# Quarter times in the scheduler of a woven attention kernel, and two tokens to a partition

## The chip, the core and the metric

The kernel runs on one core of one Trainium2 chip. It is one launch, and the metric is the device time of that launch in microseconds (us). The time before is 2787.61 us, the median of three runs (2787.22 to 2788.68).

A core has five engines that run side by side and meet at semaphores: TensorE (PE) multiplies matrices and writes to PSUM, VectorE (DVE) and ScalarE (ACT) do elementwise work and read PSUM, GpSimd (POOL) does elementwise work in SBUF, and SyncE (SP) issues DMAs here. The program fixes the order of the instructions of each engine.

## What is computed

The input `x` has 16 batches of 256 tokens of width 256. Four steps are added to it one after the other, each preceded by a conditioning step:

```python
x = x + attn0(cond(x, fside, fside, braak_embed, stage))     # cross attention, then 16 heads of width 16, causal
x = x + ffn0(cond2(x, category, W, b))                       # own weight per batch, then fp4-quantized gate/up/down
x = x + attn1(diffuse(x, zX, zY, zR))                        # reaction-diffusion, then 16 heads of width 64
x = x + moe(cond2(x, expert, ...))                           # MLP, then 8 experts, top 2, and a shared one

def diffuse(y, zX, zY, zR):                # y: tokens x features, edges reflected
    lap_x = y[:, left] - 2 * y + y[:, right]          # along the features
    lap_y = y[above, :] - 2 * y + y[below, :]         # along the tokens
    return zX * lap_x + zY * lap_y + zR * y * (1 - y)
```

`attn0` rotates queries and keys and takes the softmax of 256 x 256 causal scores per head. `attn1` first normalizes each token, then works in two segments of 128 tokens; each head has 16 extra keys and values beside the 128 of its segment. All is in fp32.

## The kernel before

The program has two parts. `woven` covers everything up to `attn1`; `mixture` covers the experts and isn't touched by the change.

**Streams.** In `woven`, each stage is a Python generator (`stage_a`, `stage_e`, `stage_f`, `stage_g`, `stage_p`, `stage_d`, `stage_v` and some that prepare weights). A generator yields operations in its own order; it can also yield a condition on the counters in `g.done` ("batch b has left stage D"), or a `Want`, a request for one of the free PSUM tiles. There are four `single` tiles of one bank and two `pair` tiles of two banks. The stages work on different batches at the same time:

- `stage_a`: cross attention, the projection of queries, keys and values (`project_heads`), and `heads_maximum`, which finds each query's largest score and stores it in `qpad`.
- `stage_e`: `heads_exponential` (scores again, with the maximum folded in, and the exponential into `b_e`), `heads_values`, then the output projection through `b_oT`, added to `x`.
- `stage_f`: the quantized feed-forward. `stage_d`: `diffuse`, the normalization and the transposed tokens `e_zT`.
- `stage_p`: projections of `attn1` for four heads at a time. `stage_g`: `scores4`, their scores and softmax into `f_prob`. `stage_v`: `values4`, the weighted values into `f_oT` and their projection, added to `x`.

**The planner.** `weave` runs while the program is built. It keeps, for each engine, the time at which it will be free, and for each tile when it was last written and read. In each turn it looks at the next operation of every stream, works out when it could start (`ready`), and issues the earliest one; ties go to the stream that stands first in the list (a, e, gate, up, down, f, g, p, d, v). The costs are constants in the code, such as `COSTS`, and for TensorE the formulas in `Unit.cost`. An operation of TensorE from another stream than the last one counts as 0.1 us later (`TURN`), so that a stream keeps TensorE while it has work ready. So the planner fixes the order of each engine's instructions; the chip's semaphores decide when they run.

**Narrow products.** TensorE's array has 128 rows. Most products use all of them ("wide"). Three groups contract over 32 rows or fewer ("narrow"), and their operands lie in one of four quarters of the rows, 0 to 31, 32 to 63 and so on:

- the maximum group of `heads_maximum`: 4 products into `pair` from `b_qkT`, 16 rows
- the exponential group of `heads_exponential`: 4 products into `pair` from `b_qS` and `b_qkT`, 17 rows
- the score group of `scores4`: 8 products into `pair` from `keys` and `f_q`, 32 rows

Each group handles two heads, so two quarters in turn: `j0 = 0` is quarters 0 and 1, `j0 = 2` quarters 2 and 3. Per batch there are eight groups of each kind. Each takes one of the two `pair` tiles and gives it back when VectorE and ScalarE have read it. The planner before gives a narrow product a cost of `max(0.155, t / 2)` and treats TensorE as one resource.

Products that write 32 or 64 columns (`heads_values`, the values in `values4`) are a third kind. An fp32 product appears as two MATMUL records in the trace.

**Tokens.** A batch of `x` lies in SBUF as `[128, 2, 256]`: partition p holds token p and token 128 + p. `diffuse` computes the token Laplacian as a product with a 256 x 256 table `lap`: for each half of the tokens, two wide products of 256 columns. `copy_` offers an operation to ScalarE and to VectorE, whichever the planner finds earlier.

In the profile, nearly all instructions of the woven part bear L162, the line in `Unit` that makes the call; they are told apart by the tiles that they write and read.

Of the kernel before, what the change touches and what calls it, by code (L numbers as in the profile page):

```python
# [19 lines left out]
P = 128  # L20
# [106 lines left out]
HOP = 0.15  # L127
LANDING = 4.5
TURN = 0.1
GAP = 0.6  # L130
# [6 lines left out]
def row_size(ap):  # L137
    return math.prod(ap.shape[1:])


# [7 lines left out]
class Unit:  # L148
# [17 lines left out]
    def cost(self, fn, outs, ins):  # L166
        if self.name == "SP":
            return 0.06
        if self.name == "PE":
            if fn == "transpose":  # L170
                return 0.12
            lhsT, rhs = ins
            rows, cols, t = lhsT.shape[0], row_size(lhsT), row_size(rhs) / 570

            if rows <= 64:
                return max(0.155 if rows <= 32 else 0.19, t / 2)
            return max(t / 3.5, 0.08) if cols <= 32 else max(t / 2, 0.13) if cols <= 64 else t
        fixed, each = COSTS[self.name]
        n = max(row_size(x) for x in outs[:1] + ins)
        if fn == "reciprocal":  # L180
            each = 0.006
        return fixed + each * n + (0.3 if len(outs) > 1 else 0)


def weave(streams):
# [4 lines left out]
    free, written, read, rings = {}, {}, {}, {}  # L190
    turn = None
    names = lambda aps: [x.tensor.name for x in aps]

    def ready(op, engine):
# [4 lines left out]
        for x in op.outs:  # L199
# [7 lines left out]
            for p in before:  # L207
                if p and not p[1] == engine == "SP":
                    t = max(t, p[0] + (HOP if p[1] != engine else 0.0))
        return t  # L210

    def issue(op, choice, start):
        engine, cost, call = choice
        free[engine] = start + cost
        end = start + cost + (LANDING if engine == "SP" else 0.0)
        for n in names(op.ins):
            if end > read.get(n, (0.0, engine))[0]:
                read[n] = (end, engine)
# [13 lines left out]
    while waiting:  # L232
        best, moved = None, False
        for rank, w in enumerate(waiting):
# [15 lines left out]
            for c in op.choices:  # L250
                start = max(ready(op, c[0]), free.get(c[0], 0.0))
                if c[0] == "PE" and w is not turn:
                    start += TURN
                key = (start + (GAP if op.filler else 0.0), rank, c[1])
                if best is None or key < best[0]:
                    best = (key, w, c, start)
        waiting = [w for w in waiting if w[0] is not None]
        if best is not None:
# [4 lines left out]
            else:  # L263
                issue(w[1], c, start)
                if c[0] == "PE" and not w[1].filler:
                    turn = w
            w[1] = None
# [127 lines left out]
def stage_e(g):  # L395

    for b in range(g.B):
# [16 lines left out]
        for c in range(2):  # L414
            for st in range(2):
                yield g.pe.transpose(pt[:, c, st * P : (st + 1) * P], o[:, st, c * P : (c + 1) * P], g.ident)
        yield copy_(g, oT, pt)
        g.singles.append(both)
# [5 lines left out]
        g.singles.append(both)  # L424
        g.done["A"] = b + 1


def fetch_a(g, b):
# [11 lines left out]
    yield g.sp.dma_start(out=f, in_=a["fside_BxSxS_0"][b].rearrange("(c p) d -> p c d", p=P))  # L440
    yield g.sp.dma_start(out=g.x[b], in_=a["x"][b].rearrange("(c p) d -> p c d", p=P))

# [370 lines left out]
def stage_p(g):  # L813
    k, a = g.k, g.a
    yield lambda: g.done["A"] > 0 and g.done["W"] == 3
    g.lap, op = load(g, g.w, "lap", [P, 2, S], a["lap"])
    yield op
    g.z = []
    for n in ("condB_zX", "condB_zY", "condB_zR"):
        t, op = load(g, g.w, n, [P, g.B], a[n].unsqueeze(0).to_broadcast([P, g.B]))  # L820
        g.z.append(t)
        yield op
    g.gn, op = load(g, g.w, "g", [P, 2], a["g"])
    yield op
# [60 lines left out]
def diffuse(g, b):  # L885

    zx, zy, zr = (z[:, b : b + 1] for z in g.z)
    y = g.x[b]
    one = yield from single(g, y)
    ply = one.rearrange("p (s d) -> p s d", s=2)  # L890
    for st in range(2):
        yield from mm_(g, ply[:, st, :], [(g.lap[:, c, st * P : (st + 1) * P], y[:, c, :]) for c in range(2)])
    lx, u = tile_l(g, [P, 2, D], "e_lx"), tile_l(g, [P, 2, D], "e_u")
    yield g.pool.tensor_tensor(lx[:, :, 1 : D - 1], y[:, :, 0 : D - 2], y[:, :, 2:D], ALU.add)
    yield g.pool.tensor_tensor(lx[:, :, 0:1], y[:, :, 1:2], y[:, :, 1:2], ALU.add)
    yield g.pool.tensor_tensor(lx[:, :, D - 1 : D], y[:, :, D - 2 : D - 1], y[:, :, D - 2 : D - 1], ALU.add)
    yield g.dve.tensor_scalar(u, y, -1.0, 1.0, ALU.mult, ALU.add)
    yield g.dve.scalar_tensor_tensor(u, y, zr, u, ALU.mult, ALU.mult)
    yield g.dve.scalar_tensor_tensor(lx, y, -2.0, lx, ALU.mult, ALU.add)
    yield g.dve.scalar_tensor_tensor(u, lx, zx, u, ALU.mult, ALU.add)  # L900
# [15 lines left out]
    for c in range(2):  # L916
        yield g.act.activation(zT[:, c, :], pt[:, c, :], AF.Copy, scale=g.gn[:, c : c + 1])
    g.singles.append(one)
# [48 lines left out]
def stage_v(g):  # L967

    for i in range(4 * g.B):
# [4 lines left out]
        if n == 3:  # L974
            yield g.sp.dma_start(out=g.k.xd[b].rearrange("(s p) d -> p s d", p=P), in_=g.x.pop(b))
            g.done["L"] = b + 1
# [37 lines left out]
def values4(g, n, b, prob, pm, v, wo):  # L1014
# [19 lines left out]
    oT = tile_l(g, [P, 2, S], "f_oT", 2)  # L1034
    yield copy_(g, oT, po)
    g.singles.append(one)
    if n % 2 == 1:
# [3 lines left out]
        for st in range(2):  # L1041
            yield g.pe.transpose(pt[:, st * P : (st + 1) * P], pm[:, st].rearrange("p j n -> p (j n)"), g.ident)
        yield copy_(g, ppT, pt)
        g.singles.append(one)
# [508 lines left out]
```

## Time and profile before

| | |
|---|---|
| median of the runs | 2787.61 us |
| the profiled execution | 2794.98 us |
| its span, first to last instruction | 2793.3 us |
| woven part, to the last projection of `attn1` | about 1799 us |
| TensorE busy | 2701.6 us (97%) |
| VectorE, ScalarE, GpSimd busy | 1434.2, 934.3, 856.5 us |
| MATMUL records | 15999 |
| mean granted TensorE clock | 0.977 |
| `x,lap` products: records, mean | 128, 381 ns |
| `keys,f_q`: records, mean | 2048, 294 ns |
| `b_qkT` into `pair`, both widths: records | 1024 |
| `b_qS,b_qkT`: records | 1024 |
| `f_oT` copies on ScalarE: count, median | 59, 585 ns |

Busy times of TensorE overlap and their ends are modelled, so work on TensorE is best read from the distance between the starts of instructions. A row of a timeline gives the start in us from the beginning, the modelled time to the end of the last one in the row, the engine, the line, the operation, what is written and read, the rows and columns used, the shape that streams through, and the count. A row of groups gives the shapes, the count, the total time and the mean of one, and then the engine's idle time before them and what ended it.

### The profile page before, as it was taken

The numbers are of one execution on the slowest core, as the hardware profiler recorded it, in microseconds if no ns is written. First come the engines' busy times: TensorE is split into PE (matmuls) and PEld (weight loads), VectorE is DVE, ScalarE is ACT, GpSimd is POOL, SyncE is SP. The second block draws the span as 40 slices with busy tenths as digits, with TensorE's granted clock in tenths as the row PEclk, the third lists the DMA queues.
The fourth block names the chain that finished last, engine by engine and source line by source line (L and its number), as shares of the span: only waits on it lengthen the run. The fifth ranks groups of instructions, "written<-read, shape, count | busy, mean of one in ns | idle before, by whom it ended". The sixth has DMA issues, their size and how long they took to land. (4 is left out here: it accounts for less than half of the span.)

```text
span 2793.3 us, 42335 instructions
## 1 busy us (share of the span) xinstructions
PE 2701.6 (97%) x15999; PEld 2045.2 (73%) x15999; DVE 1434.2 (51%) x3113; ACT 934.3 (33%) x2418; POOL 856.5 (31%) x1030
## 2 busy tenths in 40 slices
PE   7999999999999999999999999799999999999999
PEld 5666777777777777777777778555566888888866
DVE  6456776776776776776777776433340000000023
ACT  2223334333333333333333334333222222222221
POOL 4323344434444334334434344223330000000035
PEclk7879999999999999999999999899999999999999
DMA  3122032322222222222221223241112455555523
GB/s 113 58 65 87 25 99 83 94 72 70 94 73 71 93 73 71 93 74 69 93 75 64 77 83 95 75 125 50 50 39 74 139 195 193 187 196 198 198 84 106
DMA packets 196526, 270.39 MB, mean 97 GB/s; under 512 B 34912, under 2 KB 167264, under 8 KB 186976
## 3 DMA queue, kind: packets, MB, share of 16 engines
q1 hardware_dynamic: 190176, 250.87, 28.0%
q0 software_dynamic: 6144, 16.79, 2.0%
q8 instruction: 128, 2.10, 0.3%
q14 instruction: 78, 0.64, 0.1%
HBM read 207.05 MB, written 60.56 MB: 96 GB/s over the span
## 5 line engine op out<-in xcount | busy, mean ns | idle before, releaser
L162 ACT ACTIVATE f_prob<-pair,f_stat 128x144 f32<-128x144 f32 x512 | 190.3, 377 | 225.6 <-DVE f_stat L162 171.8
L162 DVE TENSOR_TENSOR pair<-pair,mask 128x256 f32<-128x256 f32 (+1 forms) x384 | 198.4, 517 | 124.3 <-PE pair L162 93.1
L1192 POOL DMA_INDIRECT got<-osort,pos_o x64 | 62.1, 971 | 628.0 <-ACT hT L1125 585.3
L1174 ACT ACTIVATE ehT<-bank,own_b 128x256 f32<-128x256 f32 x280 | 132.5, 473 | 349.1 <-PE bank L49 349.1
L162 PE MATMUL single<-e_zT,wq 128*128 128x256 f32 x1024 | 249.3, 386 | 0.0
L49 PE MATMUL bank<-ysT,w 128*128 128x256 f32 x1120 | 247.5, 379 | 0.2 <-ACT ysT L113 0.2
L49 PE MATMUL bank<-w,ehT 128*128 128x256 f32 x1120 | 247.5, 379 | 0.0
L49 PEld LDWEIGHTS bank<-ysT,w 128*128 128x128 f32 x1120 | 212.7, 190 | 29.4 <-ACT ysT L113 0.5
L49 PEld LDWEIGHTS bank<-w,ehT 128*128 128x128 f32 x1120 | 210.2, 190 | 27.2
L162 PEld LDWEIGHTS single<-e_zT,wq 128*128 128x128 f32 x1024 | 186.8, 191 | 33.5 <-issue 4.3
L162 PE MATMUL pair<-keys,f_q 32*128 32x144 f32 x2048 | 159.8, 294 | 0.2 <-ACT f_prob L162 0.2
L162 ACT ACTIVATE b_e<-pair 128x768 f32<-128x768 f32 x128 | 103.6, 809 | 163.4 <-PE pair L162 152.8
L162 PEld LDWEIGHTS pair<-keys,f_q 32*128 32x128 f32 x2048 | 132.4, 184 | 27.7 <-issue 22.8
L162 POOL TENSOR_SCALAR_AFFINE_SELECT b_e<-b_e 128x512 f32<-128x512 f32 x128 | 83.1, 649 | 216.8 <-ACT b_e L162 216.1
L1182 DVE TENSOR_TENSOR eo<-bank,eb 128x512 f32<-128x512 f32 x35 | 24.2, 692 | 234.4 <-PE bank L49 234.4
L162 POOL TENSOR_TENSOR keys<-f_t,f_t 128x256 f32<-128x256 f32 x128 | 94.5, 751 | 150.1 <-DVE f_t L162 145.7
L162 PE MATMUL single<-wo,f_oT 128*128 128x256 f32 x512 | 130.2, 387 | 9.0 <-ACT f_oT L162 8.6
L162 DVE TENSOR_REDUCE qpad<-pair 128x2 f32<-128x256 f32 (+1 forms) x256 | 131.0, 554 | 4.4
L162 DVE TENSOR_TENSOR x<-x,single 128x512 f32<-128x512 f32 (+1 forms) x112 | 67.6, 604 | 121.3 <-PE single L162 121.2
L162 PE MATMUL pair<-b_qkT 16*128 16x128 f32 (+1 forms) x1024 | 123.0, 362 | 4.7 <-ACT b_qkT L162 3.3
L162 POOL TENSOR_TENSOR f_q<-f_t,f_t 128x256 f32<-128x256 f32 x128 | 93.4, 749 | 110.2 <-DVE f_t L162 108.3
L162 POOL TENSOR_TENSOR f_prob<-f_prob,f_stat 128x1024 f32<-128x1024 f32 x64 | 125.8, 1965 | 0.0
(294 smaller groups left out, 5255.2 us busy)
## 6 DMA issues: line engine op xcount, KB each, us to landing
w<-in_w SPq DMA_DIRECT2D x70, 1024.0 KB, 5.2
ysort<-zero SPq DMA_DIRECT2D x32, 1024.0 KB, 7.8
wq<-in_w_qk SPq DMA_DIRECT2D x128, 256.0 KB, 4.5
wv<-in_w_v SPq DMA_DIRECT2D x64, 256.0 KB, 4.3
wo<-in_w_out SPq DMA_DIRECT2D x64, 256.0 KB, 3.3
ys<-ysort SPq DMA_DIRECT2D x35, 256.0 KB, 2.7
osort<-eo SPq DMA_DIRECT2D x35, 256.0 KB, 5.4
eb<-in_b SPq DMA_DIRECT2D x35, 128.0 KB, 5.2
```

What stands on the lines that cost most here:

```text
L49: nc.tensor.matmul(out, lhsT, rhs, start=start and i == 0, stop=stop and i == last)
L162: return Op([(self.name, self.cost(fn, outs, aps), lambda: call(*args, **kw))], outs, aps)
L1174: nc.scalar.activation(hT[:, f, :], ph, AF.Gelu_apprx_tanh, bias=b1[:, f : f + 1])
L1182: nc.vector.tensor_tensor(o, po, b2.unsqueeze(1).to_broadcast([P, 2, D]), ALU.add)
L1192: nc.gpsimd.indirect_dma_start(out=g, out_offset=None, in_=k.osort[:, :], in_offset=bass.IndirectOffsetOnAxis(ap=r.pos_o[:, i, t : t + 1], ...
```

## The change

It has two parts, and they don't need each other.

**The planner** keeps a time for each of the four quarters. A narrow product costs TensorE `SIDE` = 0.105 us, whatever its width, and keeps its own quarter for `0.08 + width / 600`; it can't start before its quarter is free. A wide product can't start before all four are free, and sets all four to its end. A product of 64 rows now counts as a wide one. When the last product was narrow, a narrow one from another stream is no longer put back by `TURN`. A `Want` is never put back by it. Waits of TensorE on TensorE are left out in `ready`.

**The tokens** 2p and 2p + 1 lie in partition p. The loads and stores of `x` follow (`"(p c) d"`). Neighbours of even tokens are then the odd tokens of the same partition and of the one before, and the other way round: `lap` becomes two bidiagonal tables of 128 x 128, built on GpSimd from the identity, and the token Laplacian takes one product a half. The terms with -2 and the reaction are gathered: `nzr` is -zR and `zc` is zR - 2 (zX + zY), so that u = y (nzr y + zc). Where transposed tokens have to be in their order, or the other order, the copies out of PSUM go with a step of two (`twined`, `untwined`, `by_token`).

```diff
+SIDE = 0.105
+def rows_of(op):
+    if len(op.ins) < 2 or op.ins[0].shape[0] > 32:
+        return None
+    return op.ins[0].start_partition() // 32, 0.08 + row_size(op.ins[1]) / 600
...
-            if rows <= 64:
-                return max(0.155 if rows <= 32 else 0.19, t / 2)
+            if rows <= 32:
+                return SIDE
...
-    turn = None
+    quarters = [0.0] * 4
+    turn, narrow = None, False
...
-                if p and not p[1] == engine == "SP":
+                if p and not (p[1] == engine and engine in ("SP", "PE")):
...
+        if engine == "PE":
+            part = rows_of(op)
+            if part:
+                end = quarters[part[0]] = start + part[1]
+            else:
+                quarters[:] = [end] * 4
...
-                if c[0] == "PE" and w is not turn:
-                    start += TURN
-                key = (start + (GAP if op.filler else 0.0), rank, c[1])
-                if best is None or key < best[0]:
-                    best = (key, w, c, start)
+                part = None
+                if c[0] == "PE" and c[2]:
+                    part = rows_of(op)
+                    start = max(start, quarters[part[0]] if part else max(quarters))
+                    if w is not turn and not (part and narrow):
+                        start += TURN
+                found.append([start + (GAP if op.filler else 0.0), rank, c[1], w, c, start, part])
+        if found:
+            x = min(found, key=lambda x: x[:3])
+            best = (x[:3], x[3], x[4], x[5])
...
-                    turn = w
+                    turn, narrow = w, rows_of(w[1]) is not None
...
-        yield copy_(g, oT, pt)
+        yield copy_(g, twined(oT), untwined(pt))
...
+def untwined(t):
+    return t.rearrange("p c (t r) -> p c r t", r=2)
+def twined(t):
+    return t.rearrange("p c (r t) -> p c r t", r=2)
...
-    yield g.sp.dma_start(out=g.x[b], in_=a["x"][b].rearrange("(c p) d -> p c d", p=P))
+    yield g.sp.dma_start(out=g.x[b], in_=a["x"][b].rearrange("(p c) d -> p c d", p=P))
...
-    g.lap, op = load(g, g.w, "lap", [P, 2, S], a["lap"])
-    yield op
+    g.lap, one = g.w.tile([P, 2, P], F32, name="lap"), g.ident
+    for r, dst, end in ((0, 1, 0), (1, 0, P - 1)):
+        cols = g.lap[:, r, dst : dst + P - 1]
+        yield g.pool.tensor_tensor(cols, one[:, 0 : P - 1], one[:, 1:P], ALU.add)
+        yield g.pool.tensor_tensor(g.lap[:, r, end : end + 1], one[:, end : end + 1], one[:, end : end + 1], ALU.add)
...
+    zc = g.w.tile([P, g.B], F32, name="zc")
+    yield g.dve.tensor_tensor(zc, g.z[0], g.z[1], ALU.add)
+    yield g.dve.scalar_tensor_tensor(zc, zc, -2.0, g.z[2], ALU.mult, ALU.add)
+    yield g.dve.tensor_scalar(g.z[2], g.z[2], -1.0, None, ALU.mult)
...
     for st in range(2):
-        yield from mm_(g, ply[:, st, :], [(g.lap[:, c, st * P : (st + 1) * P], y[:, c, :]) for c in range(2)])
+        yield g.pe.matmul(ply[:, st, :], g.lap[:, st, :], y[:, 1 - st, :], start=True, stop=True)
...
-    yield g.dve.tensor_scalar(u, y, -1.0, 1.0, ALU.mult, ALU.add)
-    yield g.dve.scalar_tensor_tensor(u, y, zr, u, ALU.mult, ALU.mult)
-    yield g.dve.scalar_tensor_tensor(lx, y, -2.0, lx, ALU.mult, ALU.add)
+    yield g.dve.tensor_scalar(u, y, nzr, zc, ALU.mult, ALU.add)
+    yield g.dve.tensor_tensor(u, y, u, ALU.mult)
...
-        yield g.act.activation(zT[:, c, :], pt[:, c, :], AF.Copy, scale=g.gn[:, c : c + 1])
+        by_token = zT[:, c, :].rearrange("p (t r) -> p r t", r=2)
+        yield g.act.activation(by_token, pt[:, c, :].rearrange("p (r t) -> p r t", r=2), AF.Copy, scale=g.gn[:, c : c + 1])
...
-            yield g.sp.dma_start(out=g.k.xd[b].rearrange("(s p) d -> p s d", p=P), in_=g.x.pop(b))
+            yield g.sp.dma_start(out=g.k.xd[b].rearrange("(p s) d -> p s d", p=P), in_=g.x.pop(b))
...
-    yield copy_(g, oT, po)
+    yield copy_(g, twined(oT), untwined(po))
...
-        yield copy_(g, ppT, pt)
+        rows = lambda t: t.unsqueeze(1)
+        yield copy_(g, twined(rows(ppT)), untwined(rows(pt)))
```

## The prediction

> **What bounds the kernel now.** I read the page's busy times and clock first, then equal stretches of the woven part, then TensorE's timeline over one batch.
>
> ```profile
> PE 2701.6 (97%) x15999; PEld 2045.2 (73%) x15999; DVE 1434.2 (51%) x3113; ACT 934.3 (33%) x2418; POOL 856.5 (31%) x1030
> ...
> PEclk7879999999999999999999999899999999999999
> ```
>
> TensorE is busy for 97% of the span, no other engine for more than about half. The first digits of the clock are low: up to about 315 us the streams fill up and TensorE runs partly at half speed. The woven part ends at about 1799 us; the rest, some 993 us, isn't touched by the diff.
>
> ```profile
> 578.00:682.50 104.50, 102.73 (x734) 77.93 (x733) 75.95 (x154) 40.98 (x120) 41.95 (x52) 1.00 0.24 79
> 682.50:787.00 104.50, 102.73 (x734) 77.92 (x733) 75.95 (x154) 40.99 (x120) 41.95 (x52) 1.00 0.25 79
> ```
>
> The columns are the stretch, its length, then busy time of PE, PEld, DVE, ACT and POOL. From 473.5 to 1518.6 us the copies into `b_oT`, one a batch, stand 104.5 us apart: ten equal batches, full clock. VectorE has 28 us of each free, so here TensorE's own work is the time.
>
> ```profile
> 1052.24 0.92 PE L162 MATMUL pair<-b_qkT 16*128 16x128 f32 x8
> 1053.09 3.05 PE L162 MATMUL single<-downT,d_hT 128*128 128x256 f32 x12
> ...
> 1056.08 0.38 PE L162 MATMUL pair<-b_qkT 16*128 16x128 f32 x2
> 1056.10 0.48 PE L162 MATMUL pair<-b_qS,b_qkT 17*128 17x256 f32 x2
> ...
> 1056.95 1.45 PE L162 MATMUL single<-gateT,c_yT 128*128 128x352 f32 x4
> ...
> 1061.91 0.92 PE L162 MATMUL pair<-b_qS,b_qkT 17*128 17x256 f32 x8
> 1062.76 1.45 PE L162 MATMUL single<-upT,c_yT 128*128 128x352 f32 x4
> ...
> 1066.52 0.92 PE L162 MATMUL pair<-b_qkT 16*128 16x128 f32 x8
> 1067.28 0.82 PE L162 MATMUL pair<-b_qS,b_qkT 17*128 17x256 f32 x8
> 1068.03 1.99 PE L162 MATMUL single<-e_zT,wq 128*128 128x256 f32 x8
> ...
> 1089.33 1.89 PE L162 MATMUL single<-x,lap 128*128 128x256 f32 x8
> 1091.16 0.92 PE L162 MATMUL pair<-b_qS,b_qkT 17*128 17x256 f32 x8
> ```
>
> Starts are measured, ends modelled, so only starts are used. A fp32 product leaves two MATMUL records. There are three kinds of narrow group: a maximum group (`b_qkT`, 4 products), an exponential group (`b_qS,b_qkT`, 4) and a score group (`keys,f_q`, 8). Each uses two quarters, rows 0 to 63 or 64 to 127, in turn. The reader is to see three prices:
> - Alone, a maximum or exponential group takes 0.85 us to the next wide product (1053.09 - 1052.24; 1062.76 - 1061.91), a score group 1.18 (1010.08 to 1011.26). Its surroundings pay about 0.2 us more: the first narrow product comes 0.09 us late after a wide one, and the second wide product behind it 0.10 late.
> - Two adjoining groups on different quarters: at 1056.08 the maximum group and, 0.02 us later, the exponential group run side by side, together 0.87 us. That saves 0.85 + 0.85 - 0.87 + 0.2 = **1.03 us**. An exponential and a score group at 1083.37 do the same (wide at 1084.57).
> - Two adjoining groups on the same quarters, 1066.52 to 1068.03: 1.51 us. That saves 1.70 - 1.51 + 0.2 = **0.39 us**.
>
> In each steady batch the 24 narrow groups stand in 20 runs: four joins, two of either kind.
>
> **The change, part by part.**
>
> *Layout: the Laplacian.* Four wide products a batch become two. The eight records at 1089.33 are 0.216 us apart; four go: 0.864 us a batch, straight off TensorE. In the first two batches TensorE still waits for other engines and the gain is likely hidden, so 14 x 0.864 = **-12.1 us**. The least I allow is 10 x 0.864 = 8.6.
>
> *Layout: VectorE and GpSimd.* One 0.75 us operation of `diffuse` goes and one of 0.82 becomes a plain product of some 0.69: about -0.9 of 76 us a batch. VectorE isn't the bound: 0, and with the cover gone it would still be a gain. The `lap` table costs GpSimd four small additions once (2 x 0.43 + 2 x 0.24 = 1.3 us, from its rows of 128 x 128 and 128 x 2), at about 99 us, where GpSimd is a third busy; it replaces one DMA that took 3.6 us to land. Three tiny VectorE operations for `zc`, once. All 0. The DMAs of `x` and `xd` keep their number, bytes and queue; DMA is at 0.24 here.
>
> *Layout: copies with a step of two.* Per batch, one `b_oT`, four `f_oT` and two half-size `f_ppT` copies read PSUM at every second value; two `e_zT` halves write SBUF so. No row shows a step in PSUM. The nearest rows have it in SBUF, on VectorE:
>
> ```profile
> L162 DVE TENSOR_TENSOR b_t<-b_qk,sin 128x256 f32<-128x256 f32 x32 | 13.8, 432 | 0.0
> L162 DVE TENSOR_TENSOR vpad<-pair,bqkv 128x256 f32<-128x256 f32 x32 | 13.3, 415 | 0.0
> ```
>
> The first reads and writes every second value, the second packed runs: 432 against 415 ns, no penalty worth the name. By them the `f_oT` copy stays at 585 ns on ScalarE and the term is 0. The Trainium skill, "SBUF — State Buffer", section "Specifications (TRN2)", speaks against the change: it gives SBUF lines of 16 bytes that need two hits for full rate, and PSUM lines of only 8, so every second fp32 would be a new line. If that doubled the moving part, a copy would take (585 - 376) / 256 x 512 = 0.42 us more (from the 512- and 256-wide copies), for the PSUM ones some 2.5 us of ScalarE's 63 free ones a batch. TensorE has waited for `f_oT` 8.6 us in the whole run, at 13 places; each 0.42 longer is 5.5 us. I take the row, 0, and keep +5.5 for the range.
>
> *Scheduler.* Nothing new runs on the chip; the order changes. `ready` no longer counts a product after a product, a `Want` no longer pays `TURN`, and a narrow product behind a narrow one of another stream doesn't either, while a wide one must wait until all quarters are free. So whatever narrow group is ready while another runs is joined to it. What a join is worth stands above; two things have to be chosen.
>
> First, whether mixing products *inside* a join adds anything. The Trainium skill, "TensorE: Matmul & The Clock Gate", section "Part 3: Packing small matmuls — row/col tiling", has matmuls start and end strictly in program order. By that rule the two different-quarter joins would today run one after the other, taking 1.51 us like two on the same quarters, and mixing would give 1.51 - 0.87 = 0.64 us for each: 1.3 a batch, 17 us over 13 batches. But the old scheduler issues the turn's own four products before the other stream's (they lack the 0.1 of `TURN`), and the trace has the second group start 0.02 us after the first: the chip overlaps them already. I take the row: **0 for mixing itself**, -17 kept for the range.
>
> Second, how many joins are added. Upper estimate: from the time when a group's input and PSUM pair are there (input copy's end, last reader's end) to its start, medians are 0.6 to 1 us for maximum, 1.1 to 2.4 for exponential groups; I take 1.2, and 0.8 for the run itself. Groups of the other two streams come at 16 / 104.5 = 0.153 a us: 24 x 0.153 x 2.0 = 7.3 joins, 3.3 more than now. Lower: I walk through the batch at 1000 us by hand. The score group that starts at 1071.60 had its keys at 1059.45 and a free pair from 1058.81; it would join the exponential group at 1061.91 on other quarters (1.03). The one at 1048.31 would join that at 1046.87 on the same (0.39). But moving the first one may undo the join at 1083.37: one to two joins net. I take 2.4, half of each kind, 0.71 us on average: 1.7 us a batch. Over 13 batches that is **-22 us**. A late product has a cost too: both PSUM pairs fill at once. The score group's pair is held 5.5 to 6.3 us, the other kinds' 1.8 to 2.8; what is late next is the maximum and exponential groups' own stream. It has room: the streams finish attention at 996.0 and start the next batch's heads only at 1013.1, 17 us later. So 0 for that, and a rival below.
>
> **Sum.** -12.1 + 0 + 0 - 22 = -34 us. The profiled execution took 2794.98 us for a span of 2793.3, so it would take 2761; it lies 7.4 above the median of the runs, so the median goes from 2787.61 to **2753 us**, 1.2% faster.
>
> **Rivals.**
> - *Joins become the rule* (15%). Early `Want`s keep both pairs filled; nearly all groups pair up, 6 more joins a batch at 0.71 and 13 batches: -55, with the Laplacian -67, or 2720; with the mixing term, 2703. For it: from a group's first product to its last reader, all users together hold the two pairs 1627 of 2 x 1799 us, 45%. Against: score groups mostly wait for the value products, so they aren't there to be joined.
> - *Only the Laplacian counts* (12%). New joins undo old ones: -12, 2776. For it: the walk above.
> - *It cancels* (5%): within 0.2%, about what a measurement tells from no change, so 2782 to 2793.
> - *Slower: the pair wait becomes the cycle* (13%). Joined groups hold both pairs; each of the 16 maximum and exponential groups of a batch waits for one. It decides once their chain grows by over 17 us a batch, 1.1 us a group. At 1.2 us each, a little under half a maximum group's hold, the batch is 16 x 1.2 - 17 = 2.2 us longer, whatever TensorE saves: 13 x 2.2 = +29, so 2816. Against: in today's joins the pairs are released after 2.73, 1.85 and 5.5 us, as alone.
>
> **How the numbers follow.** The forecast has 55%; its own range is 2735 to 2768 (joins from 1 to 4 a batch, copies up to +5.5, and some 8 us either way in the half-clock start). Faster: 55 + 15 + 12 = 82%. Same 5%, slower 13%. Range for 8 in 10: from 2709, which leaves out the far end of the first rival, to 2794, which leaves out nearly all of the slower case.
>
> **What would show it.** Right: `x,lap` at 64 records instead of 128; 101 to 103 us between `b_oT` copies; 16 to 19 narrow runs a batch; `f_oT` still near 585 ns. Wrong: copies near 1 us with TensorE waiting behind them; more TensorE gaps before narrow groups with a batch over 104.5; a start-up longer than 473 us before batches become equal; or side-by-side groups that take over 1.2 us.

## The result, and the profile after

The changed kernel took 2807.68 us (median of four runs, 2805.14 to 2811.92) against 2787.64 for the kernel before: ratio 1.0069, with a 95% interval of 1.0057 to 1.0081. The forecast was 2753, in a range of 2709 to 2794. The change made the kernel 20 us slower.

The page of the changed kernel, its busy times and its row of the clock:

```profile
PE 2694.7 (96%) x15907; PEld 2029.6 (72%) x15907; DVE 1421.9 (51%) x3106; ACT 926.9 (33%) x2412; POOL 866.6 (31%) x1034
...
PEclk7779999999999999999999999999999999999999
```

(L170 is the line that was L162.) TensorE is busy 7 us less in the profiled execution (11 us longer than the one before), so the time went into idle stretches, and part of its busy time is half clock. Its groups show the two parts of the layout as forecast:

```profile
L170 ACT COPY f_oT<-single 128x512 f32<-128x512 f32 x52 | 30.5, 586 | 40.9 <-PE single L170 40.4 <-ACT b_qS L170 0.4
L170 PE MATMUL single<-x,lap 128*128 128x256 f32 x64 | 17.4, 394 | 0.0
```

The Laplacian has 64 records, half of before, and the copy with a step of two takes 586 ns, as before (585). Next, stretches from one copy into `b_oT` to the next: length, then busy time of PE, PEld, DVE, ACT and POOL, the granted clock, DMA share and GB/s.

```profile
681.50:804.80 123.30, 119.51 (x853) 91.15 (x854) 84.09 (x173) 48.63 (x149) 49.24 (x60) 0.99 0.22 68
804.80:908.20 103.40, 96.99 (x667) 70.98 (x668) 68.31 (x137) 35.36 (x104) 38.64 (x46) 0.95 0.27 87
1118.00:1222.10 104.10, 101.57 (x729) 76.19 (x728) 74.45 (x155) 39.88 (x117) 42.24 (x52) 1.00 0.25 80
1222.10:1327.80 105.70, 103.17 (x729) 77.36 (x728) 74.46 (x155) 39.93 (x117) 42.25 (x52) 0.98 0.25 79
```

Where there were ten equal batches of 104.5 us, there are now batches of 92 to 123 us that settle at 104.1 to 105.7. The last two stretches have the same number of TensorE's records; the second of them has one stretch of 3.4 us at half clock, and is 1.6 us longer. What TensorE waited for, in the table of waits (total us, times, longest):

```profile
PE pair L170 <- POOL a_qT L170: 8.6, 3, 7.8
PE single L170 <- DVE a_e L170: 8.5, 12, 1.1
...
PE single L170 <- DMA wq<-in_w_qk: 5.6, 2, 4.0
PE single L170 <- POOL d_h L170: 4.9, 13, 0.6
```

Before:

```profile
PE pair L162 <- POOL a_qT L162: 11.8, 11, 8.1
PE single L162 <- ACT f_oT L162: 8.6, 13, 0.7
...
PE single L162 <- POOL d_h L162: 3.4, 5, 1.1
```

The pairs, which one rival named, are not what it waits for more (8.6 us for `a_qT` in `pair`, after 11.8). New are the waits of wide products into `single` tiles: 8.5 us for `a_e`, and a weight DMA that once kept TensorE for 4.0 us, up to 811.8 us; the half clock of the second stretch above sets in during it, at 810.1 us. Over the ten batches of the next table alone, the waits listed for TensorE add up to 17.0 us before and 29.2 after.

Cutting the span by the copies into `b_oT` (the fifth, the fifteenth) and the last product of the woven part gives four pieces. "Half clock" is the time in the clock's records at less than full speed.

| profiled execution | before | after |
|---|---|---|
| start, to the fifth copy | 473.5 | 485.9 |
| half clock in it | 102.4 | 116.1 |
| ten batches | 1045.1 | 1050.2 |
| half clock in them | 0 | 17.1 |
| tail of the woven part | 280.9 | 277.6 |
| experts | 993.8 | 990.8 |

So instead of the 34 us forecast off the batches and the tail, +1.8 us there, and +12.4 us in the start. The experts, which the change doesn't touch, were 3 us shorter.

The ten batches hold 17.1 us of half clock that the ten before don't have. At 1.6 us for each 3.4 us of it, as in the stretch at 1222.1, that is an estimated 8 us: at full clock they would have taken some 1042 us, 3 less than before. `e14`, told below, has the same order and 10.2 us of half clock there, and took 1047.0.

The next table sorts the ten batches' TensorE time, a batch, from the start of one product to the start of the next. A wide product counts for its usual spacing. The column "same order" belongs to a run told below (`e13`).

| us a batch | before | same order | after |
|---|---|---|---|
| wide products | 68.62 | 67.77 | 67.28 |
| narrow groups | 21.04 | 21.04 | 20.53 |
| products into 32 or 64 columns | 7.41 | 7.71 | 7.73 |
| switches between wide and others | 4.93 | 4.93 | 5.15 |
| waits | 2.49 | 2.44 | 4.31 |
| sum | 104.5 | 103.9 | 105.0 |
| runs of narrow groups | 20.0 | 20.0 | 18.4 |

Narrow groups gained 0.5 us and wide ones 1.3; waits took 1.8 back, the other rows 0.5. Two things are mixed in. Of the wide gain, 0.4 is work that now lies outside the ten batches: they have 60 fewer records of 256 columns, and only 40 of these are the Laplacian's. And the column "after" holds the half clock, an estimated 0.8 us a batch; the waits listed for TensorE rose by 1.2 us a batch ((29.2 - 17.0) / 10).

### The profile page after: what moved, and what is told of

It is laid out like the page before. It is cut to its first block, busy times and chain, and to the rows that moved or that the text cites. A ratio compares the mean times of both kernels' runs of the same rounds, so it can differ in the third digit from the quotient of the medians.

```text
span 2804.4 us, 42152 instructions
## 1 busy us (share of the span) xinstructions
PE 2694.7 (96%) x15907; PEld 2029.6 (72%) x15907; DVE 1421.9 (51%) x3106; ACT 926.9 (33%) x2412; POOL 866.6 (31%) x1034
## 5 line engine op out<-in xcount | busy, mean ns | idle before, releaser
L170 ACT ACTIVATE f_prob<-pair,f_stat 128x144 f32<-128x144 f32 x512 | 191.3, 379 | 303.0 <-DVE f_stat L170 292.9
L170 PE MATMUL single<-e_zT,wq 128*128 128x256 f32 x1024 | 252.0, 390 | 5.7 <-DMA wq<-in_w_qk 5.6
L170 DVE TENSOR_TENSOR pair<-pair,mask 128x256 f32<-128x256 f32 (+1 forms) x384 | 197.7, 516 | 117.7 <-PE pair L170 93.6
L170 PEld LDWEIGHTS single<-e_zT,wq 128*128 128x128 f32 x1024 | 188.7, 193 | 39.8 <-issue 8.2
L170 POOL TENSOR_SCALAR_AFFINE_SELECT b_e<-b_e 128x512 f32<-128x512 f32 x128 | 85.8, 670 | 286.7 <-ACT b_e L170 285.7
L170 PE MATMUL pair<-keys,f_q 32*128 32x144 f32 x2048 | 161.5, 293 | 0.4 <-ACT f_prob L170 0.3
L170 ACT ACTIVATE b_e<-pair 128x768 f32<-128x768 f32 x128 | 103.7, 810 | 158.3 <-PE pair L170 138.6
L170 PEld LDWEIGHTS pair<-keys,f_q 32*128 32x128 f32 x2048 | 135.0, 185 | 26.5 <-issue 20.0
L170 POOL TENSOR_TENSOR keys<-f_t,f_t 128x256 f32<-128x256 f32 x128 | 94.6, 759 | 153.4 <-DVE f_t L170 152.6
L170 POOL TENSOR_TENSOR f_q<-f_t,f_t 128x256 f32<-128x256 f32 x128 | 97.3, 777 | 137.9 <-DVE f_t L170 124.7
L170 PE MATMUL single<-wo,f_oT 128*128 128x256 f32 x512 | 128.8, 384 | 5.0 <-ACT f_oT L170 4.2
L170 DVE TENSOR_REDUCE qpad<-pair 128x2 f32<-128x256 f32 (+1 forms) x256 | 131.0, 554 | 4.4
L170 PE MATMUL pair<-b_qkT 16*128 16x128 f32 (+1 forms) x1024 | 126.3, 369 | 5.7 <-ACT b_qkT L170 3.7
L170 DVE TENSOR_TENSOR x<-x,single 128x512 f32<-128x512 f32 (+1 forms) x112 | 67.9, 606 | 116.8 <-PE single L170 116.8
L170 PE MATMUL single<-wv,e_zT 128*128 128x256 f32 x512 | 125.0, 388 | 1.8 <-DVE f_t L170 1.8
```

The lines of the kernel that those rows point to most:

```text
L170: return Op([(self.name, self.cost(fn, outs, aps), lambda: call(*args, **kw))], outs, aps)
```

## The experiments

Two kinds of theory stood against each other. **Theory B**: any new order loses something, because the order before is a favourable draw among the many orders that the planner's rules can give. The others lay the loss on the change itself, on one part or rule; **D** says so of the new rules as a whole, or of the quarters' times. In the expectations, **A** means the planner's part (A1: the `Want` that pays no `TURN`; A2: the mixing or the quarters' times), and **C** the copies or the new order in `diffuse`. For each kernel I give the time, the ratio to the kernel before on the same chip with its interval, and "batches + tail": the length of the ten batches and the tail of the woven part in the profiled execution (before: 1045.1 + 280.9 = 1326.0). Two executions with the same order agree in it to 1.7 us or better (before and `e4`: 1326.0 and 1325.7), so it shows the order without the start; half clock in the batches is still in it. What a kernel costs in us is its median less that of the kernel before timed beside it.

### One part alone

**`e1_layout`**: before, with all of the diff outside `Unit.cost` and `weave`, so the layout alone:

```diff
+        yield copy_(g, twined(oT), untwined(pt))
...
+        yield g.pe.matmul(ply[:, st, :], g.lap[:, st, :], y[:, 1 - st, :], start=True, stop=True)
...
```

> The kernel before with the layout part alone: two tokens to a partition, one Laplacian product a half, copies with a step of two; the planner as before. If the planner's changes cost the time (theory A), the layout is worth about its Laplacian: 2770 to 2780 us. If the copies or the new order of the diffuse stage cost it (theory C), 2795 us or more. If any change of the plan moves the time by some 10 to 20 us in either direction (theory B), it can be anywhere from 2765 to 2800 and says little alone.

Measured: 2787.34 us, 0.9993 (0.9985 to 1.0002), batches + tail 1326.6. The 12 us of the Laplacian didn't come, in a plan that differs from the one before in most places. C, which would have had 2795 us or more, is out.

**`e2_planner`**: after, with the old layout, so the planner alone:

```diff
-        yield copy_(g, twined(oT), untwined(pt))
+        yield copy_(g, oT, pt)
...
-        yield g.pe.matmul(ply[:, st, :], g.lap[:, st, :], y[:, 1 - st, :], start=True, stop=True)
+        yield from mm_(g, ply[:, st, :], [(g.lap[:, c, st * P : (st + 1) * P], y[:, c, :]) for c in range(2)])
...
```

> The kernel before with the planner's part alone: quarter times, mixing, Wants without TURN; tokens and Laplacian as before. Theory A: slower than before by the changed kernel's loss and the Laplacian's gain together, 2815 to 2825 us. Theory C: 2765 to 2785 us. Theory B: no relation to the other run, and the sum of the two differences from before does not give the changed kernel's +20 us.

Measured: 2831.39 us, 1.0146 (1.0129 to 1.0162), batches + tail 1353.4 with a tail of 303.8. The planner's part alone costs 42 us; with a layout that alone does nothing, it costs 20. The parts don't add.

### One rule alone

**`e3_want_turn`**: after, with `TURN` for a `Want` again:

```diff
-                    if w is not turn and not (part and narrow):
-                        start += TURN
+                if c[0] == "PE" and w is not turn and not (part and narrow):
+                    start += TURN
```

> The changed kernel, but a Want of another stream pays TURN again, as before. If early claims of PSUM tiles make TensorE wait (theory A1), it returns to 2785 us or less. If mixing itself or the quarter times do it (theory A2), it stays within 5 us of 2807. Theory B: anywhere, with other waits in another place.

Measured: 2803.79 us, 1.0043 (1.0031 to 1.0056): the start 23 us shorter than the changed kernel's (462.9), the tail 23 longer (300.2). The time is what A2 expected (within 5 us of 2807), not A1 (2785 or less).

**`e5_want`**: before, with only that rule of the change.

```diff
-                if c[0] == "PE" and w is not turn:
+                if c[0] == "PE" and c[2] and w is not turn:
```

> The kernel before with one rule of the planner changed: a Want never pays TURN. Theory A1 (early claims cost): the start gets longer, fewer of the TensorE filler products are placed there (74 against 90) and more of it runs at half clock; 2795 to 2810 us, with the first b_oT copies at 100 us and later. Theory D (the quarter times cost): within 5 us of before.

Measured: 2820.03 us, 1.0133 (1.0107 to 1.0159), batches + tail 1357.0. In `e3` the rule taken away brought 4 to 6 us, here the rule alone costs 33.

**`e6_mix`**: before, with only the rule that a narrow product behind a narrow one pays no `TURN`.

```diff
-                if c[0] == "PE" and w is not turn:
+                part = c[0] == "PE" and c[2] and rows_of(op)
+                if c[0] == "PE" and w is not turn and not (part and narrow):
...
```

> The kernel before with one rule changed: a narrow product behind a narrow one of another stream pays no TURN; costs as before, no quarter times. If joins are worth what the trace of before shows, some more of them and 2775 to 2787 us. Theory B (each new plan is a new draw): 2765 to 2810.

Measured: 2805.62 us, 1.0077 (1.0051 to 1.0103), batches + tail 1351.6. Narrow runs fell to 18.6 a batch, as joins should make them, and batches alternate between 102.2 and 108.9 us. But the joins are of the poorer kind. Call a join side by side when its run is over 0.6 us shorter than its groups would be alone (0.85 or 1.18 us each): the ten batches before have 20 such among 40 joins, those of `e6` none among 54, and narrow time is 0.9 us a batch longer.

**`e7_quarters`**: before, with the quarters' times, `SIDE` and the shorter `ready` of the change, but `TURN` paid as before.

```diff
...
+                if c[0] == "PE" and c[2]:
+                    part = rows_of(op)
+                    start = max(start, quarters[part[0]] if part else max(quarters))
                 if c[0] == "PE" and w is not turn:
                     start += TURN
...
```

> The kernel before with the quarter times and SIDE, and TensorE's waits on itself left out, but TURN for everybody as before: no mixing. Theory D (the quarter times cost: a wide product is planned behind the quarters, so a group that is not joined counts longer, and the order that follows makes TensorE wait): 2820 us or more. Theory A1: within 5 us of before.

Measured: 2808.27 us, 1.0076 (1.0056 to 1.0095), batches + tail 1350.9: even batches of 105.8 us, and less than D's 2820.

**`e8_rows64`**: before, with only the price of products with 64 rows as in the change.

```diff
-            if rows <= 64:
-                return max(0.155 if rows <= 32 else 0.19, t / 2)
+            if rows <= 32:
+                return max(0.155, t / 2)
```

> The kernel before with only the cost of a 64-row product changed, from 0.22 to 0.45 us (two products a batch of 256 columns, and none else). It changes no rule. Theory B: moves by 5 us or more, to either side. Theories A1 and D: within 5 us of before.

Measured: 2817.87 us, 1.0105 (1.0087 to 1.0123), batches + tail 1361.4. One price costs more than the whole change. `e7` contains this price among its edits and costs less (21 us against 31); the two `TURN` rules singly cost 33 and 19, and all together, in `e2`, 42.

**`e4_noise`**: before, with `LANDING = 4.6` in place of 4.5.

> The kernel before with one constant of the planner shifted without meaning: LANDING 4.6 instead of 4.5. The PE order differs in 217 listed lines. Theory B: moves by 3 us or more. Theory A: within 3 us of 2787.6.

Measured: 2788.25 us, 0.9995 (0.9986 to 1.0004). This tells nothing on theory B: the order came out the same as before on every engine, not with the differences that the expectation counted. It is of use as a second execution of that order.

### Meaningless prices

To see what a draw is worth, a constant is moved by a hair, under the old rules (`e9`, `e10`, `e15`) and under the new (`e11`, `e12`, `e16`). (What two of the expectations call the charge for a change of tiling mode is `TURN`, the charge for a change of stream.)

```diff
-TURN = 0.1                                # e9, e11
+TURN = 0.11
...
-HOP = 0.15                                # e10, e12
+HOP = 0.16
...
-"ACT": (0.16, 0.00083)                    # e15
+"ACT": (0.165, 0.00083)
...
-LANDING = 4.5                             # e16
+LANDING = 4.6
```

> The kernel before, its rules untouched, with the charge for a change of tiling mode at 0.11 us in place of 0.10: no rule changes, only a price by a hundredth of a microsecond, and the plan written from it differs from batch to batch. Theory B (the order before is a favourable draw among orders that the same rules give, and any new draw loses some of it): 2795 to 2825 us, like the five orders of the earlier runs that really differ. Theory D (the new rules are what costs; orders by the old rules are all about as good): within 5 us of 2787.

> The kernel before with the hop from one engine to another priced at 0.16 us in place of 0.15, nothing else. A second draw by the old rules. Theory B: 2795 to 2825 us. Theory D: within 5 us of 2787.

> The kernel before with ScalarE's fixed price at 0.165 us in place of 0.160, no rule changed; over a third of the rows of TensorE's order differ from the order before. A third draw by the old rules with a meaningless price. Theory B (the order before is a favourable draw): 2797 to 2822 us. Theory D (orders by the old rules are all about as good): within 5 us of 2787.

> The changed kernel with the charge for a change of tiling mode at 0.11 us in place of 0.10: another draw by the new rules with the new layout. Theory B: anywhere in 2785 to 2825 us, as likely below the changed kernel's 2807.7 as above, and about 10 us under the draws by the old rules on the average, for the halved Laplacian and the few joins that have the same worth in any order. Theory D: 2803 to 2815 us, that is near the changed kernel and well above the draws by the old rules.

> The changed kernel with the hop between engines at 0.16 us in place of 0.15: a second draw by the new rules. Theory B: 2785 to 2825 us, scattered as the draws by the old rules are. Theory D: 2803 to 2815 us.

> The changed kernel with the time of a landing DMA priced at 4.6 us in place of 4.5; some 110 rows of TensorE's 2900 stand elsewhere. Theory B, where also a few moved rows can cost or bring as much as the whole change: 2795 to 2820 us, and not the changed kernel's 2807.7 to within 1 us. If the new rules themselves set the time: 2806 to 2810 us.

| | rules, layout | us | ratio (95%) | batches + tail |
|---|---|---|---|---|
| `e9_before_turn` | old | 2818.82 | 1.0094 (1.0077 to 1.0111) | 1365.9 |
| `e10_before_hop` | old | 2802.50 | 1.0046 (1.0031 to 1.0061) | 1343.1 |
| `e15_before_act` | old | 2810.59 | 1.0076 (1.0059 to 1.0093) | 1355.4 |
| `e11_after_turn` | new | 2800.11 | 1.0030 (1.0018 to 1.0042) | 1335.1 |
| `e12_after_hop` | new | 2812.18 | 1.0070 (1.0053 to 1.0087) | 1342.5 |
| `e16_after_landing` | new | 2789.44 | 1.0007 (0.9989 to 1.0024) | 1321.0 |

A hundredth of a microsecond or less in a price, with no rule changed, costs the kernel before 13 to 29 us; one rule of the change alone cost 19 to 33. That is theory B, and D is out. One steady batch of `e9_before_turn`, in the same columns as above:

```profile
908.50:1015.80 107.30, 103.69 (x734) 78.94 (x732) 76.49 (x152) 40.10 (x121) 41.68 (x52) 1.00 0.24 77
```

It has the work of the batch before and takes 107.3 us; by the same sorting, 1.9 of the 2.8 us more are waits. Narrow time is 1.0 us longer: none of the 60 joins in the ten batches of `e9` is side by side. So the favour of the order before lies in part in which groups it happens to join. Under the new rules the draws lie on both sides of the changed kernel's 1327.8: `e16`, with some 110 of TensorE's 2900 rows elsewhere, took 18 us less: in the profiles 6.8 in batches + tail (some 5 of it by 10 us less half clock, at the rate above), and 13.1 in the start, of which more below.

### The order held

**`e13_same_order`**: the new layout in the old order. What the layout drops stays in the plan and isn't issued:

```diff
+def planned_only(op):
+    op.choices = [c[:2] + (lambda: None,) for c in op.choices]
+    return op
...
         yield g.pe.matmul(ply[:, st, :], g.lap[:, st, :], y[:, 1 - st, :], start=True, stop=True)
+        yield planned_only(g.pe.matmul(ply[:, st, :], g.lap[:, st, :], y[:, st, :], start=True, stop=True))
...
```

> The layout of the change (two tokens to a partition, two Laplacian products an image in place of four) in exactly the order of the kernel before: the planner prices the two dropped products and the dropped VectorE operation as if they were there, and nothing is issued for them; the new matrix is written where the old one was loaded, and the three small VectorE operations ahead of the first diffusion. On TensorE nothing differs but the 32 products. If step (a) of the prediction is right and the halved Laplacian was lost to a new order alone: 2775 us (2787.6 less 12), within 2772 to 2779. If the products saved are taken back by the waits behind them, in this order too: 2784 to 2788 us. If the step-of-two copies or the new operations cost something: above 2788 us.

Measured: 2785.37 us, 0.9987 (0.9976 to 0.9999), that is 0.3 to 6.7 us faster than before; ten batches of 103.9 us. A gain, and not 12 us. The timeline of `e13_same_order` shows where the rest of a batch's 0.86 us goes (start, length, engine, operation, and the idle time before it with what ended it):

```profile
978.75 2.34 POOL L162 TENSOR_TENSOR f_prob<-f_prob,f_stat 128x1024 f32<-128x1024 f32 x1
...
981.05 1.03 POOL L162 TENSOR_TENSOR e_lx<-x 128x508 f32<-128x508 f32 x1
982.04 0.63 POOL L162 TENSOR_SCALAR_AFFINE_SELECT b_e<-b_e 128x512 f32<-128x512 f32 x1
982.40 0.14 PEld L162 LDWEIGHTS single<-b_e,vpad 128*32 128x32 f32 x4 [0.33 <-POOL e_lx L162]
...
982.72 0.58 PEld L162 LDWEIGHTS single<-b_e,vpad 128*32 128x32 f32 x12 [0.17 <-POOL b_e L162]
```

The same place before:

```profile
989.82 0.63 POOL L162 TENSOR_SCALAR_AFFINE_SELECT b_e<-b_e 128x512 f32<-128x512 f32 x1
...
991.17 0.37 PEld L162 LDWEIGHTS single<-b_e,vpad 128*32 128x32 f32 x12 [0.33 <-issue]
```

Before, GpSimd had masked `b_e` at 990.45 and TensorE came for it at 991.17. With the shorter Laplacian ahead of it TensorE comes 0.9 us earlier in the batch (98.8 instead of 99.7 us after the copy into `b_oT`), and GpSimd, whose rows follow one another, is then still at the mask behind `e_lx`. The 0.7 us of room are used up, and 0.3 us become a wait inside this group: the row of the 32-column products in the table above.

**`e14_two_fillers`**: the changed kernel in its own order, with each filler of the start issued twice. (On the DMA queue two writes of zeros move forward.) A filler is a product of the identity with itself, yielded by `stage_fill` until the first batch has left `stage_a`; the planner issues it where TensorE has nothing better for 0.6 us.

```diff
+        name, cost, call = op.choices[0]
+        op.choices = [(name, cost, lambda call=call: (call(), call()))]
         op.filler = True
```

> The changed kernel in exactly its own order, each of the start-up's filler products issued twice (304 records in place of 152), so that TensorE stands still less while the first image is under way. If the changed kernel's longer start-up comes from TensorE standing idle and so from more time at half clock: the half-clock time of the start falls from 116 us to about 90, the start from 485.9 us to about 475, and the kernel from 2807.7 to about 2797. If the clock is not what lengthens the start: 2806 to 2815 us, the doubled fillers getting in the way.

Measured: 2796.98 us, 1.0035 (1.0021 to 1.0048), 10.7 us less than the changed kernel; half clock in the start 61.4 us, the start 470.8. It looks like the clock's doing. Whether the fillers brought it, or another draw of the clock, this run can't tell, and three others make the reading narrower. `e16` has the changed kernel's TensorE order up to 807 us, single fillers included, and its start took 472.8 us too, with 78.5 us at half clock. The stretches of the changed kernel:

```profile
0.00:55.00 55.00, 37.64 (x200) 30.45 (x201) 34.30 (x67) 11.68 (x25) 27.22 (x40) 0.82 0.45 143
55.00:100.00 45.00, 43.67 (x244) 31.80 (x243) 21.36 (x48) 14.86 (x31) 13.99 (x20) 0.57 0.03 10
```

and of `e16_after_landing`:

```profile
0.00:55.00 55.00, 37.48 (x206) 30.78 (x208) 34.29 (x69) 12.14 (x26) 27.45 (x41) 0.88 0.43 143
55.00:100.00 45.00, 38.43 (x288) 28.58 (x285) 24.35 (x59) 16.38 (x34) 15.58 (x24) 0.89 0.18 52
```

The ninth column is the granted clock: 0.57 against 0.89 from 55 to 100 us. The same products stand less than 0.4 us apart in the two traces at 50 us, 1.2 at 55 and 11.3 at 97 us, and nothing in the order of any engine differs by then. So this part of the 20 us is what the clock granted in those executions.

**`e17_same_order_fillers`** and **`e18_landing_fillers`**: `e13` and `e16` with the same doubled fillers.

> The layout in exactly the order of the kernel before, as in the run with that order, and each filler product of the start-up issued twice besides (360 records in place of 180). If the clock of the start-up costs in this order what it cost in the changed kernel's (10.7 us for 55 us less at half clock, when the start had 116 us of it): the start here has 92 to 102 us at half clock, some 40 to 50 us of it go, and the kernel comes to 2776 to 2779 us. If that gain was special to the changed kernel's order: 2784 to 2788 us.

> The changed kernel in the order that a landing DMA priced at 4.6 us gave (2789.4 us with single fillers), each filler issued twice besides. By the same reckoning: about 8 us less, 2779 to 2784 us, below the kernel before and the changed one. If the clock is not what is gained: 2788 to 2792 us.

Measured: 2785.86 us, 0.9989 (0.9982 to 0.9995), and 2789.82 us, 1.0015 (1.0003 to 1.0026). Both are where they were with single fillers (2785.37, 2789.44), though the half clock in the start fell, from 92.2 to 75.1 us and from 78.5 to 61.4. The gain forecast for both didn't come: if fillers helped at all, it was only in a start that was granted little clock, as the changed kernel's was. `e17`, like `e13`, is faster than the kernel before, by about 3 us.

## Why the prediction was wrong

**The step that failed is the sum itself:** "-12.1 + 0 + 0 - 22". It takes the profiled order, puts the edits into it and lets all else stand. But the edits went into a planner that chooses greedily, and every choice shifts the later ones; what was compared was one order with another, not one order with a shorter one. In its terms: the joins brought 0.3 us a batch where 1.7 were counted; the waits, counted at nothing, grew by 1.2 us a batch or more; and the clock, which stood in the range alone, took an estimated 8 us of the ten batches and lengthened the start. Eight orders with the old layout (`e2`, `e5` to `e10`, `e15`) have 1343.1 to 1365.9 us for batches + tail, the order before 1326.0: it lies 17 us below the best of the eight and 29 below their mean, 1355 (`e10`, the best, has an estimated 3 us of half clock in it). A forecast of "-34 from here" would have had to ask first where "here" stands.

*Laplacian, -12.1.* Right in the work: 64 records, wide products 0.85 us a batch less (0.864 forecast). Wrong to call it "straight off TensorE": in an unchanged order 0.6 of it reached the batch, the rest became a wait behind GpSimd, and the kernel gained about 3.6 us, not 12.

*VectorE and GpSimd, 0, and copies, 0.* Right. Copies of `f_oT` took 586 ns on ScalarE; those of `b_oT` on VectorE 692 where they had taken 681; the halves of `e_zT` 489 for 472. The penalty for lines of 8 bytes that the prediction drew from the Trainium skill, "SBUF — State Buffer", "Specifications (TRN2)", and the +5.5 us that it kept for it, didn't show here.

*Mixing inside a join, 0.* Right. In the changed kernel's timeline the two groups are interleaved by the planner, and cost what they cost when the planner issued them one after the other:

```profile
968.50 0.38 PE L170 MATMUL pair<-b_qkT 16*128 16x128 f32 x2
968.51 0.50 PE L170 MATMUL pair<-b_qS,b_qkT 17*128 17x256 f32 x2
...
968.71 0.50 PE L170 MATMUL pair<-b_qkT 16*128 16x128 f32 x4
...
968.83 0.39 PE L170 MATMUL pair<-b_qS,b_qkT 17*128 17x256 f32 x2
...
969.38 0.56 PE L170 MATMUL single<-gateT,c_yT 128*128 128x352 f32 x1
```

From 968.50 to the wide product at 969.38 it is 0.88 us, and was 0.87 at 1056.08 before. Strict program order, as the Trainium skill's "TensorE: Matmul & The Clock Gate", "Part 3: Packing small matmuls — row/col tiling", has it, isn't what either trace shows.

*Joins, -22.* Wrong in size. Runs of narrow groups fell from 20.0 to 18.4, two thirds of the 2.4 forecast and inside "16 to 19". But narrow time fell by 0.51 us and switches rose by 0.22: 0.3 us a batch, where 1.7 was forecast. The price of 0.71 was that of a join for which nothing else moves, and it took half of the joins to be side by side. Of the 16 joins that the ten batches gained, 6 are side by side; the other 10 saved 0.2 us or nothing, and the 0.2 us of surroundings that every join was to save didn't come.

*Both pairs filling at once, 0.* The pairs are not where it waits. What I didn't price is that a product that is moved forward moves another back: the waits rose from 2.5 to 4.3 us a batch in the sorted table, and by 1.2 us a batch in the list of waits: above all for `a_e` (8.5 us in the ten batches, none before) and for weights in `wq` (5.6, none before), while those for `f_oT` fell from 6.9 to 0.6. This, the half clock in the batches, which the sum had at nothing too, and the two items above leave the +1.8 us for batches and tail. Without the half clock an estimated 6 us of gain would stand there, of the 34.

*The start.* "Some 8 us either way" was in the range but not in the sum. It came to +12.4 in the profiled execution, and `e16` shows that one and the same order of TensorE can give or take as much. All four timed runs of the changed kernel had a mean granted clock of 0.971 to 0.974; later runs of the kernel before that took 2787 to 2788 us had 0.980 to 0.982. Among runs of one kernel, a thousandth less goes with 1.6 to 2.7 us more, by straight lines through the kernels with seven runs or more (`e16`: 2780.58 us at 0.982, 2802.34 at 0.973; the changed kernel: 2805.14 at 0.974, 2811.92 at 0.971). By such slopes the nine thousandths or so between the two kernels go with 14 to 24 us, most or all of the 20. `e14`, with the same order and more fillers, had 0.981 on the mean where the kernel before beside it had 0.980, and took 8 us longer than that (2796.98 against 2789.00). So at equal clock the changed order costs something between nothing and 10 us. How much of the lower clock belongs to the changed order, and how much to those four executions, stays open: the changed kernel itself wasn't timed again.

Two of the signs named for "wrong" came true, a start over 473 us and batches over 104.5 on the average with TensorE gaps. No rival had the mechanism. The slower one had the nearest time, 2816, but by pairs; "new joins undo old ones" had the nearest thought, and kept the -12.

*What stays open.* Whether the new rules are worth anything on the average. But for the order before itself, orders with the old layout lie at 1343 to 1366 us whether the rules are old (`e9`, `e10`, `e15`), partly new (`e5` to `e8`) or new (`e2`, 1353); those with the new layout at 1321 to 1349 with old rules (`e1`) or new ones (`e11`, `e12`, `e16`, the changed kernel, and `e3` but for one rule). That speaks for the layout rather than the rules. But the draws are few, and no experiment added joins to a fixed order.

## What to carry to other kernels

When an edit goes through a planner that works greedily, first move a meaningless constant a few times and see how far the time scatters: here by 13 to 29 us in 2788, more than most terms of the sum. A product taken off the busiest engine is worth only what the next engine in line has in hand at that place; read its margin in the timeline (0.7 us here, of 0.86 saved) before multiplying by the batches. To test such an edit, hold the order fixed and let the planner price what is no longer issued.

## What the runs showed of the hardware

The start-up can differ by over 11 us between executions of the same order. Between the changed kernel and `e16` so much had opened by 97 us, nearly all of it after 55 us, where the clock was granted at 0.57 in one and 0.89 in the other. The profiles of the kernel before and of `e4`, with one order on every engine, differ likewise: 473.5 us with 102.4 at half clock, 469.1 with 92.2. Half-clock stretches come in multiples of about 3.4 us (3.4, 6.8, 10.2, 13.7, 20.5, 37.5), and the first of them begins at 11.3, 11.7, 12.4 or 13.7 us in different executions with the same first products. The Trainium skill, "TensorE: Matmul & The Clock Gate", section "Part 1: The HAM clock gate", has the clock decided in windows of about 3.4 us that run freely and don't start with the kernel; the traces agree with both. That less half clock, under more fillers, need not shorten an already well-clocked start (`e17`: 17 us less of it, and the start went from 468.0 to 475.2) I had not expected; the cause is open.

TensorE starts a later group's products on free quarters before an earlier group's remaining ones, so a planner that interleaved them by hand gained nothing at the place shown: 0.88 against 0.87 us.
